# Graph layer of a two-block network: VectorE's copy into the padded stationary matrices moved behind the maxima over the neighbours in the second layer

## The chip, the cores and the metric

The kernel runs on one core of a Trainium2 chip. The metric is the device time of one execution in microseconds, the median over several runs. Before the change it is 1098.5 us (three runs, 1095.35 to 1098.69).

The engines are named as the profile names them: PE is TensorE's matmul and PEld its weight load, DVE is VectorE, ACT is ScalarE, POOL is GpSimd, SP is SyncE, which only issues DMAs here.

## The reference, cut to what matters

The program is a chain of six residual parts on an activation `x` of 2 x 64 x 1024: a quantised product, a state-space block, a feed-forward part with routed low-rank additions, a graph network over point clouds, a masked linear layer and a gated feed-forward part. The change lies in the graph network, `_L1_xattn_ref`. There are two clouds (the batch) of 1024 points, and two layers of this form:

```python
def _get_graph_features(feats, inds_list, perm, W_lin, b_lin, k=K):
    ...
    for inds in inds_list:
        neigh = gather(feats, inds)
        gf = jnp.concatenate([jnp.broadcast_to(center, (B, N, k, C)), neigh - center], axis=-1)
        per_method.append(gf)
    ...
    scores = jnp.einsum('bihd,bjhd->bhij', qh, qh) / np.float32(np.sqrt(headdim))
    attn = jax.nn.softmax(scores, axis=-1)
    out = jnp.einsum('bhij,bjhd->bihd', attn, qh).reshape(B * N, k, total)
    fused = out @ W_lin.T + b_lin
    return fused.reshape(B, N, k, 128)
...
g2 = _get_graph_features(feats1.transpose(0, 2, 1), inds_list, perm2, W_lin2, b_lin2)
h2 = jnp.einsum('oc,bnkc->bonk', W_conv2, g2)
h2 = _lrelu(_instance_norm(h2, (2, 3)))
feats2 = h2.max(axis=-1)
```

Every point has K = 10 neighbours in each of four orders of the points along curves. For every point the 10 neighbours attend to one another, the result goes through two linear maps (64 output channels in the first layer, 128 in the second), is normalised over all points and neighbours of a cloud, and the largest value over the neighbours is kept.

## The kernel before, in words

**Tiling.** The graph network works through *items*. An item is 48 neighbouring points of one cloud and one layer (the last item of a cloud is smaller: 16 points, or half the columns). A cloud has 22 items; the order is layer 1 cloud 0, layer 1 cloud 1, layer 2 cloud 0, layer 2 cloud 1, 88 items in all. Points are packed three at a time into blocks of 32 columns (30 used), so a full item has 16 blocks and its attention scores are one 128 x 512 tile.

**The software pipeline.** All engine queues in this part are in the order in which the program issues instructions; no scheduler reorders them. The function `iteration(i)` (L1281) issues one step, in which up to seven items are in work at different stages. A step issues, in this order:

- on POOL, `edges` of item i+2 (L999): the differences between neighbours and centre points, `x`, from the arrays `win` and `cen`, 128 x 960 elements; just before or after it stand gathers (`sl`, L948), indirect DMAs that POOL issues to fetch rows of the next cloud;
- `apart` of item i+1 (L1011 and L1013): `x` is copied into `xz`, a matrix padded with zeros, in which the two 64-row halves stand apart so that it can serve TensorE as a stationary matrix. Half 1 is copied by DVE in layer 2 (L1011), and by ACT in layer 1 except for the very first item; half 0 is copied by ACT (L1013), later in the step;
- `turn` of item i-2 (L1048): DVE transposes the normalised attention weights `e` in 32 x 32 blocks into `at`. It needs POOL's product of an earlier step (L1044);
- `collect` of item i-4 (L1113, L1115): DVE takes statistics (`st`) and maxima over the neighbours (`hm`) from the PSUM tile `pt`, which TensorE's back-transposition (L1102) wrote at the end of the step before. `pt` has one buffer, so the next back-transposition must wait for the maxima. After a cloud's last item `finish` adds the normalisation to the plan;
- `exponentials` of item i-1 on ACT (L1037), `scores` of item i on PE (L1019, L1022);
- `normalize` of item i-1: DVE sums the exponentials into `z` (L1042) and takes the reciprocal (L1043), and POOL multiplies `e` by it (L1044);
- `maxima` of item i: DVE takes the largest score (`mx`, L1027) and, in layer 2, subtracts it (L1030);
- `apart` half 0 of item i+1 on ACT, `attend` of item i-3 on PE (L1089, L1092) with ACT's copy `oT` (L1094), `weighted` of item i-1 on PE (L1073 in layer 2) with ACT's copies `u` (L1075), `turn_u` (L1079, layer 1 only), and `back` of item i-3 on PE (L1102).

Side work from a list with due times (`plan`, run by `todo`) is issued between these: the gathers, the placing of gathered rows (L955, L960, L965), the terms of the centre points (`crest`, `ct`, L920 and L927 on DVE), the Newton steps of a normalisation (L159 to L170), leaky ReLU (L1184), and, near the end, POOL's products that mask a weight of the next layer (L1395, `w_attn`).

**Order on DVE in one step of layer 2.** Copy (L1011), `at` (L1048), `st` (L1113), `hm` (L1115), `z` (L1042), reciprocal (L1043), `mx` (L1027), `e` (L1030), then side work. **Order on POOL.** Gather if one is due, `x` of item i+2 (L999), gather if one is due, product (L1044), masked weight if due (L1395).

**Buffers.** `x` and `xz` have four buffers each, the scores two in PSUM, `pt` one.

Of the kernel before, what the change touches and what calls it, by code (L numbers as in the profile page):

```python
# [92 lines left out]
class Kernel:  # L93
# [1093 lines left out]
    def point_cloud(self):  # L1187
        nc, tc, a = self.nc, self.tc, self.a
        with ExitStack() as es:
# [63 lines left out]
            at = lambda i: items[i] if 0 <= i < last else None  # L1253

            def todo(i):
                while plan and plan[0][0] <= i:
                    plan.pop(0)[1]()
# [16 lines left out]
            def edge(i):  # L1274
                it = at(i)
                if it:
                    it["pu"] = []
                    it["x"], it["xz"] = x16[i % len(x16)], xz[i % len(xz)]
                    self.edges(it)

            def iteration(i):  # L1281


                todo(i - 0.5)
                edge(i + 2)
                todo(i - 0.25)
                if at(i + 1):
                    self.apart(at(i + 1), 1)
                if at(i - 2):
                    self.turn(at(i - 2))  # L1290
                if at(i - 4):
                    it = at(i - 4)
                    ph, end = it["ph"], it["last"]
                    self.collect(it)
                    if end:
                        work = self.finish(ph)
                        if work:
                            plan.extend((i + k, w) for k, w in enumerate(work))
                            plan.sort(key=lambda e: e[0])
                if at(i - 1):  # L1300
                    self.exponentials(at(i - 1))
                if at(i):
                    self.scores(at(i))
                if at(i - 1):
                    self.normalize(at(i - 1))
                if at(i):
                    self.maxima(at(i))
                if at(i + 1):
                    self.apart(at(i + 1), 0)
                if at(i - 3):  # L1310
                    self.attend(at(i - 3))
                if at(i - 1):
                    self.weighted(at(i - 1))
                    self.turn_u(at(i - 1))
                if at(i - 3):
                    self.back(at(i - 3))
                todo(i)

            for i in range(-2, last + 3):
                iteration(i)  # L1320
# [8 lines left out]
            for q in range(2):  # L1329
                part(q, slice(0, P), w3, feats, start=True)  # L1330
                part(q, lo, w3a, phases[0]["out"])
                part(q, hi, w3a, phases[1]["out"])
                part(q, lo, w3b, phases[2]["out"], stop=True)
            iteration(last + 3)
            for q in range(2):
                part(q, hi, w3b, phases[3]["out"], stop=True)
# [204 lines left out]
```

## Time and profile before

One execution was profiled. It spans 1105.6 us from the first to the last instruction, and took 1107.58 us, 9 us more than the median of the runs shown; the mean granted clock of TensorE was 0.970.

| what | us |
|---|---|
| median of three runs | 1098.5 |
| profiled execution, time | 1107.58 |
| profiled execution, span | 1105.6 |
| steps that issue the 44 second-layer copies, first to last copy's start | 739.96 to 1003.49 |
| chain of waits, share of PE | 45% |
| chain of waits, share of DVE | 28% |
| chain of waits, share of POOL | 7% |
| chain of waits, share of the copy L1011 over the whole chain | 3% |

How such lines are read. A line of the groups names the source line, engine and operation, then output and inputs with their shapes, the number of instances, the busy time and the mean length of one in ns, and last the idle time of the engine in front of them with what ended most of it. A line of the timeline has the start, the length, the engine, the line, the operation and its tiles; an entry in brackets is idle time ahead of it. In a table by stretches each number is the busy time of one engine in that stretch. An instruction that stands still inside itself counts as busy.

### The profile page before, as it was taken

The numbers are of one execution on the slowest core, as the hardware profiler recorded it, in microseconds if no ns is written. First come the engines' busy times: TensorE is split into PE (matmuls) and PEld (weight loads), VectorE is DVE, ScalarE is ACT, GpSimd is POOL, SyncE is SP. The second block draws the span as 40 slices with busy tenths as digits, with TensorE's granted clock in tenths as the row PEclk, the third lists the DMA queues.
The fourth block names the chain that finished last, engine by engine and source line by source line (L and its number), as shares of the span: only waits on it lengthen the run. The fifth ranks groups of instructions, "written<-read, shape, count | busy, mean of one in ns | idle before, by whom it ended". The sixth has DMA issues, their size and how long they took to land.

```text
span 1105.6 us, 34714 instructions
## 1 busy us (share of the span) xinstructions
PE 990.0 (90%) x15287; PEld 736.7 (67%) x15287; DVE 800.3 (72%) x1667; ACT 604.7 (55%) x988; POOL 511.9 (46%) x425
## 2 busy tenths in 40 slices
PE   3899989999999999894788879889899899999997
PEld 1798949688696867453455545558777788887443
DVE  6698975776777676343588888889988689998411
ACT  6334416665756743113677767667877677775010
POOL 0010110102162446226999979888667577882000
PEclk9999999999999999895999999999999999999999
DMA  9777758695866957455031003110323200000550
GB/s 345 259 293 289 308 207 328 233 425 210 365 267 268 382 211 284 161 170 102 17 69 29 13 11 70 22 32 15 56 39 94 90 14 12 9 4 3 218 238 20
DMA packets 49027, 170.93 MB, mean 155 GB/s; under 512 B 26551, under 2 KB 27491, under 8 KB 42093
## 3 DMA queue, kind: packets, MB, share of 16 engines
q1 hardware_dynamic: 38988, 151.83, 37.0%
q10 hardware_dynamic: 3744, 12.65, 3.4%
q0 software_dynamic: 6144, 4.24, 2.2%
q8 instruction: 120, 1.97, 0.7%
q14 instruction: 31, 0.25, 0.1%
HBM read 163.48 MB, written 2.72 MB: 150 GB/s over the span
## 4 chain that ended last, share of the span: by engine, by line
PE 45%; DVE 28%; POOL 7%; ACT 7%; DMA 6%; issue 6%; ACTq 0%; DVEq 0%; SPq 0%; POOLq 0%
PE pin L369 11%; PE po L506 7%; PE misc L1073 6%; POOL sl L948 3%; DVE cpre L384 3%; PE op L1092 3%; PE sc L1422 3%; DVE xz L1011 3%; DMA sl<-src,place 2%; DMA df<-in_L_attn_mask 2%; POOL e L1044 2%; POOL x L999 2%; PE misc L1422 2%; DVE z L1042 2%; DVE mx L1027 2%
## 5 line engine op out<-in xcount | busy, mean ns | idle before, releaser
L369 PE MATMUL pin<-hT,w 128*128 128x128 f32 x2320 | 263.3, 275 | 1.2 <-issue 0.8
L369 PEld LDWEIGHTS pin<-hT,w 128*128 128x128 f32 x2320 | 261.0, 192 | 4.9 <-issue 4.2
L999 POOL TENSOR_TENSOR x<-win,cen 128x960 f16<-128x960 f32 (+1 forms) x88 | 170.3, 1935 | 4.4 <-ACT win L965 3.0
L1013 ACT COPY xz<-x 64x1024 f16<-64x1024 f16 (+1 forms) x131 | 133.6, 1020 | 15.3 <-POOL x L999 11.3
L948 POOL DMA_INDIRECT sl<-src,place x128 | 129.0, 1007 | 25.5 <-issue 14.3
L1073 PE MATMUL misc<-wz,xz 128*64 128x128 bf16 x4128 | 129.1, 220 | 6.1 <-issue 2.6
L1073 PEld LDWEIGHTS <-xz 128*64 128x64 f16 x4128 | 118.7, 110 | 18.0 <-issue 17.0
L1044 POOL TENSOR_TENSOR e<-e,z 128x512 f32<-128x512 f32 x88 | 91.0, 1034 | 76.6 <-DVE z L1043 63.4
L483 POOL TENSOR_TENSOR xc<-y,normw 128x512 f32<-128x512 f32 x8 | 8.3, 1037 | 243.4 <-DVE y L481 200.8
L1075 ACT COPY u<-misc 128x512 f32<-128x512 f32 x172 | 97.1, 587 | 32.5 <-PE misc L1073 24.3
L799 ACT ACTIVATE df<-df,neg 128x1024 f32<-128x1024 f32 x64 | 73.4, 1148 | 75.6 <-DVE df L798 66.3
L506 PE MATMUL po<-ow,xc 128*128 128x512 f32 x240 | 109.8, 611 | 0.0
L384 DVE SCALAR_TENSOR_TENSOR cpre<-craw,convw,cpre 128x126 f32<-128x126 f32 (+2 forms) x240 | 80.6, 357 | 24.3 <-ACT cpre L378 18.6
L782 POOL DMA_INDIRECT place<-cst,rank x64 | 66.2, 1035 | 51.5 <-DVE rank L804 23.7
L1092 PE MATMUL op<-u,at 128*32 128x64 f32 (+1 forms) x2752 | 84.5, 256 | 3.4 <-issue 3.1
L798 DVE SCALAR_TENSOR_TENSOR df<-hi_r,hl,lo_r 128x1024 f32<-128x1024 f32 x64 | 80.8, 1292 | 3.2 <-DMA lo_r<-rows 1.5
L506 PEld LDWEIGHTS po<-ow,xc 128*128 128x128 f32 x240 | 46.1, 197 | 53.3 <-issue 52.5
L1048 DVE STREAM_TRANSPOSE at<-e 128x512 f32<-128x512 f32 x88 | 61.1, 694 | 20.3 <-POOL e L1044 19.6
L1022 PEld LDWEIGHTS <-xz 128*64 128x64 f16 x2752 | 51.6, 114 | 34.7 <-issue 32.6
L1062 PE MATMUL misc<-x,heads 128*32 128x512 f16 (+1 forms) x1056 | 73.4, 395 | 1.2 <-issue 0.5
L1042 DVE TENSOR_REDUCE z<-e 128x16 f32<-128x512 f32 x88 | 58.0, 659 | 19.5 <-ACT e L1037 19.2
L1092 PEld LDWEIGHTS op<-u,at 128*32 128x32 f32 x2752 | 61.3, 113 | 14.1 <-issue 6.9
(364 smaller groups left out, 1557.9 us busy)
## 6 DMA issues: line engine op xcount, KB each, us to landing
w<-in_in_proj_w SPq DMA_DIRECT2D x36, 2048.0 KB
ow<-in_out_proj_w SPq DMA_DIRECT2D x16, 2048.0 KB
w<-in_L_ffn_w SPq DMA_DIRECT2D x3, 4096.0 KB
ow<-in_ctx SPq DMA_DIRECT2D x4, 1024.0 KB
w<-in_ctx SPq DMA_DIRECT2D x4, 1024.0 KB
hi_r<-rows ACTq DMA_DIRECT2D x8, 512.0 KB
lo_r<-rows ACTq DMA_DIRECT2D x8, 512.0 KB
df<-in_L_attn_mask ACTq DMA_DIRECT2D x8, 512.0 KB
```

What stands on the lines that cost most here:

```text
L369: nc.tensor.matmul(pt[:, c, :], w[:, c, kc, :], hT[:, kc, :], start=(kc == 0), stop=(kc == KC - 1))
L384: nc.vector.scalar_tensor_tensor(pv[:, :, s:], rv[:, :, :S - s], convw[:, cc + c, 3 - s:4 - s], pv[:, :, s:], ALU.mult, ALU.add)
L506: nc.tensor.matmul(st["pq"][n], st["xc"][:, 4 * q + c, :], ow[:, c, 512 * n:512 * n + 512], start=(q == 0 and c == 0), stop=(q == 1 and c ...
L798: V.scalar_tensor_tensor(df, hi_r, hl[:, 0, cc:cc + 1], lo_r, ALU.subtract, ALU.add)
L948: nc.gpsimd.indirect_dma_start(out=ph[c][:, m, :], out_offset=None, in_=ph["src"][:, :], in_offset=bass.IndirectOffsetOnAxis(ap=k, axis=0))
L999: nc.gpsimd.tensor_tensor(xv[:, :, r0:nb], over, mid, ALU.subtract)
L1013: nc.scalar.copy(dst, src)
L1042: nc.vector.tensor_reduce(z, e, AX.X, ALU.add)
L1044: nc.gpsimd.tensor_tensor(e, e, z.unsqueeze(2).to_broadcast([P, nb, 32]), ALU.mult)
L1073: nc.tensor.matmul(pu[64 * hp:64 * hp + 64, k, :], xz[:, hp, k0 + k].rearrange("p a j -> p (a j)"), wz[j][:, hp, :], start=(j == 0), stop= ...
L1075: nc.scalar.copy(u[:, k0:k0 + kb], pu)
L1092: nc.tensor.matmul(op[32 * r:32 * r + 32, q, :], it["at"][:, 4 * q + r, :], it["u"][:, 4 * q + r, :], start=False, stop=True, skip_group_c ...
```

## The change

DVE's half of `apart` is taken out of its place at the head of the step for items of layer 2 and issued after `collect` and `finish`, in front of `exponentials`. For items of layer 1 it stays where it was (there it is ACT's copy, with one exception, the very first item).

```diff
                 todo(i - 0.25)
-                if at(i + 1):
+                if at(i + 1) and at(i + 1)["layer"] == 1:
                     self.apart(at(i + 1), 1)
                 if at(i - 2):
                     self.turn(at(i - 2))
...
                             plan.extend((i + k, w) for k, w in enumerate(work))
                             plan.sort(key=lambda e: e[0])
+
+                if at(i + 1) and at(i + 1)["layer"] == 2:
+                    self.apart(at(i + 1), 1)
                 if at(i - 1):
                     self.exponentials(at(i - 1))
```

In DVE's compiled queue the 44 copies then stand behind `at`, `st` and `hm` and in front of `z`. The other instructions of DVE, and those of PE, ACT, POOL and SP, keep their order. The copy no longer carries a wait for POOL; the transposition in front of it carries one. Lines behind the inserted ones, about L1300 on, have numbers higher by 3 in the changed kernel; all the lines named above but L1395 stand before it.

## The prediction, made before the changed kernel was run

> **What bounds the kernel now.** I read the page's busy line first, then the stretches in which the second graph layer runs, then VectorE's and GpSimd's timelines inside them, and last the chain of waits. The page's first line:
>
> ```profile
> PE 990.0 (90%) x15287; PEld 736.7 (67%) x15287; DVE 800.3 (72%) x1667; ACT 604.7 (55%) x988; POOL 511.9 (46%) x425
> ```
>
> TensorE's 90% is an average. The change touches 44 copies of the second layer, started between 740 and 1003 us. Busy times there (columns: stretch, length, then PE, PEld, DVE, ACT, POOL busy, clock, DMA):
>
> ```profile
> 740.00:760.00 20.00, 17.46 (x528) 13.28 (x530) 19.11 (x36) 12.22 (x24) 18.78 (x16) 1.00 0.08 15
> 760.00:782.00 22.00, 19.25 (x577) 16.52 (x567) 21.09 (x49) 17.52 (x30) 14.76 (x12) 1.00 0.06 12
> 812.00:851.00 39.00, 36.98 (x1008) 30.93 (x1002) 34.82 (x53) 29.11 (x52) 26.34 (x20) 1.00 0.13 29
> 922.00:949.00 27.00, 26.58 (x789) 22.74 (x784) 25.33 (x44) 20.67 (x37) 25.19 (x19) 1.00 0.07 15
> 949.00:1003.00 54.00, 51.57 (x1529) 44.01 (x1526) 52.66 (x69) 38.94 (x68) 42.03 (x28) 1.00 0.02 5
> ```
>
> So TensorE is near full in some stretches (26.58 of 27) and VectorE in others (52.66 of 54). In the latter VectorE is full partly because it stands still. Groups kept apart by shape, 740 to 1003:
>
> ```profile
> L999 POOL TENSOR_TENSOR x<-win,cen 128x960 f16<-128x960 f32 x40 | 79.8, 1995 | 0.6
> L1011 DVE COPY xz<-x 64x1024 f16<-64x1024 f16 x42 | 47.6, 1134 | 1.1
> ```
>
> The copy's shortest full instances take 0.42 us, so 42 of them should take 17.6; about 30 us are waiting inside the instruction. The timeline says for whom:
>
> ```profile
> 958.02 1.05 POOL L1044 TENSOR_TENSOR e<-e,z 128x512 f32<-128x512 f32 x1
> 958.02 5.12 DVE L1011 COPY xz<-x 64x1024 f16<-64x1024 f16 x1
> 959.02 1.91 POOL L1395 TENSOR_TENSOR w_attn<-w_attn,on 128x1024 f32<-128x1024 f32 x1
> 960.89 1.96 POOL L999 TENSOR_TENSOR x<-win,cen 128x960 f16<-128x960 f32 x1
> ...
> 967.00 1.91 POOL L1395 TENSOR_TENSOR w_attn<-w_attn,on 128x1024 f32<-128x1024 f32 x1
> 967.16 2.05 DVE L1011 COPY xz<-x 64x1024 f16<-64x1024 f16 x1
> 968.88 2.15 POOL L999 TENSOR_TENSOR x<-win,cen 128x960 f16<-128x960 f32 x1
> ```
>
> Each blocked copy ends 0.30 us after a GpSimd instruction does (963.14 after 962.85; 969.21 after 968.91): it cannot run beside one. The chain of waits between 949 and 1001 goes through copy, transposition and VectorE's issue in every step, so there this blocking is the step time (6.05 us from copy to copy).
>
> **The change, part by part.** Nothing is added or removed. Forty-four copies, on VectorE alone, move behind three neighbours in its queue: the transposition of the weights (L1048), the statistics (L1113) and the maxima over neighbours (L1115). No DMA moves. The copy's own wait for GpSimd goes, since the transposition in front now waits for a later GpSimd product.
>
> Its users: TensorE's scores read it a step later. At 882.76 a copy begins whose scores begin at 889.77; 3 us later is still in time, cost nothing. TensorE's back-transposition (L1102) needs the maxima to have freed its PSUM buffer, so it may go up to one copy (0.42 to 2 us) earlier: a gain where it waited (0.2 to 0.46 us a step near 965 to 983). Queued behind the copy are now the sums z (L1042), the reciprocal and GpSimd's product (L1044), which waits for them: that decides.
>
> Where does the copy arrive? One undisturbed step, VectorE and GpSimd interleaved:
>
> ```profile
> 800.37 0.67 DVE L1042 TENSOR_REDUCE z<-e 128x16 f32<-128x512 f32 x1
> 801.47 1.05 POOL L1044 TENSOR_TENSOR e<-e,z 128x512 f32<-128x512 f32 x1 [0.33 <-DVE z L1043]
> 802.63 0.50 DVE L1011 COPY xz<-x 64x1024 f16<-64x1024 f16 x1
> 802.67 0.99 POOL L948 DMA_INDIRECT sl<-src,place  x1
> 803.14 0.71 DVE L1048 STREAM_TRANSPOSE at<-e 128x512 f32<-128x512 f32 x1
> 803.68 1.97 POOL L999 TENSOR_TENSOR x<-win,cen 128x960 f16<-128x960 f32 x1
> 804.88 0.66 DVE L1042 TENSOR_REDUCE z<-e 128x16 f32<-128x512 f32 x1
> ```
>
> Before, the copy slips in ahead of the gather (802.63 against 802.67) and takes 0.50; z to z is 4.51 us. After, transposition, statistics and maxima (0.63 + 0.55 + 0.55 us) come first, so the copy arrives at z + 4.0, inside x, which began at z + 3.31 and ends at z + 5.28. With the 0.30 us that follow a release, next z is at z + 5.60. A closed loop has come about: **z, product, gather, x, copy, z = 5.60 us**, against TensorE's own step of 5.56 (scores at 925.20 and 930.76). Where VectorE used to catch up at 4.5 us a step it no longer can; where TensorE leads, the loop just fits beside it and costs nothing.
>
> By stretches:
> - **740 to 782** (layer change; GpSimd busy 18.78 of 20). Steps were 4.1 to 5.1 us. At the first, the product ends at 741.03, the shortened collection brings the copy to about 742.33, and x starts at 742.19: it loses by 0.14 and waits to 744.17 + 0.3. The first four z, at 742.57, 746.72, 751.26 and 755.94, become 744.5, 750.1, 755.2 and 760.8 (5.6 us a step, the half-size item a little less). +4.9, of which an unblocked copy at 766.54 (0.77) returns 0.4: **+4.5**. If the copy won that 0.14 us, only each x would be 0.43 later: about +1.
> - **782 to 812**: VectorE at 5.6 us where it ran 4.5, TensorE busy 28.1 of 30 by its row: **+0.5**.
> - **812 to 851**: two copies of 2.71 and 2.72 us, blocked by gather and x, now fall free of both. TensorE has 39.0 - 36.98 = 2.0 us to give: **-2.0**, ends 0 and -3.
> - **851 to 900**: VectorE waits 0.9 to 3.0 us a step for TensorE: **0**.
> - **900 to 949**: one copy of 1.90 goes free (-1.4), given back because three steps of 4.4 to 5.0 become 5.6: **0**, ends -1.4 and +1.5.
> - **949 to 1003**: GpSimd also multiplies the masked weight (L1395). Before, the copy waited for it and got in ahead of x, though x was next (x stretched to 2.15). The loop becomes 1.10 + 1.00 + 1.87 + 1.97 + 0.33 = 6.27 us against 6.05: six steps, +1.3, and entering it +0.9: **+2.2**. The other end: the copy gets in before x, and TensorE's 5.56 takes over, -3.
> - **after 1003**: no more x; TensorE idles 1.4 of 17 us, of which half comes back: **-0.7**.
>
> Sum 4.5 + 0.5 - 2.0 + 2.2 - 0.7 = **+4.5 us**. The profiled execution spans 1105.6 us (1107.58 as timed), 9 above the median of the runs, 1098.5; the sum is a difference inside that execution, and I add it to the median: **1103.0 us**.
>
> **A rule against the row.** The last stretch hangs on who gets in when the copy arrives at z + 4.01 and the weight product ends at z + 4.01 (973.06 + 1.91 - 970.96). The Trainium skill, "SBUF — State Buffer", section "Who interferes with whom", says that VectorE and GpSimd share a port pair as an exclusive lock, and that whichever issues first holds it for its whole instruction. By it a copy pending before x goes ahead of x, a step falls to TensorE's 5.56, and the stretch gives -3: the sum would be -0.7. The rows agree with the lock, but not with first come: the copy of 958.02 was overtaken by two GpSimd instructions begun after it, and one at 791.77 lost to an x recorded 0.07 us later and took 2.34. I take the row: a near tie is lost. The same page's summary advises putting whichever of the two is off the critical path behind; here the blocked one is moved in front of what GpSimd waits for, which speaks against the change.
>
> **Rivals.**
> - Faster: the copy wins its races. Layer change +1, 812 to 851 -2, batch change -1.4, last stretch -3, end -0.7: -6, **1092.5 us**. Five copies pending during the weight product did win. The point is the order of arrival: 0.14 us earlier at the layer change, some 0.05 at the end. Against it: ordinary steps arrive 0.7 us too late.
> - No difference: TensorE's 5.56 hides the loop's 5.60 everywhere but where gains and losses cancel; **1098.5**. For it, 26.58 of 27 busy; against it, TensorE idles 5.3 of the first 42 us.
> - Slower still: two loops within 1% of each other lose slack at each uneven step (positions, centres, Newton's steps). 0.15 us in 30 more steps: +9, **1107.5**.
> - That the move is not made can be left out: VectorE's compiled queue shows it.
>
> **Numbers.** Forecast 0.45, still slower 0.17, no difference 0.18, faster 0.20. This kernel's runs spread over 0.3%, so within 3.3 us counts as the same. Almost all of the first two lie above: slower 0.60, same 0.20, faster 0.20. The stretches' ends added give about -6 and +10; cut to 8 in 10: 1093 to 1109. The forecast alone spans 1101 to 1106.
>
> **What would show it.** Right: copies of 1 to 1.6 us ending 0.3 us after an x; z to z of 5.6 in steps that took 4.1 to 4.5; 6.3 from 965 on; GpSimd's products waiting longer for the reciprocal. Wrong: copies at 0.42 with x stretched instead, steps of 5.6 in the last stretch, or TensorE waiting for the copy in the scores.

## The result, and the profile after

The changed kernel takes 1102.74 us (median of 13 runs, 1099.8 to 1115.07); the kernel before takes 1096.1 us in as many runs beside it (1092.85 to 1105.42). The ratio is **1.0065, 95% interval 1.0041 to 1.0089**: slower, by 7.1 us (4.5 to 9.8).

The execution that was profiled is the shortest of its 13 (span 1097.7 us, time 1099.8 us), while the one of before was a long one (1107.58 us). Its last sum in front of the moved copies (L1042, called z41 below) comes 9 us earlier than in before (728.20 for 737.23), by code that the change does not touch. So the two spans cannot be set against each other; the way from one sum z to another can. The busy line of the changed kernel's page:

```profile
PE 976.4 (89%) x15287; PEld 726.6 (66%) x15287; DVE 804.4 (73%) x1667; ACT 604.4 (55%) x988; POOL 511.2 (47%) x425
```

No engine's work has changed: the counts are the same, VectorE's busy time is 4.1 us higher (800.3 before). The stretches of the changed kernel that lie 9 us earlier than the first two and the last two rows shown of before; the first two are as far behind z41 as there, and hold less of the work, since the steps are longer (stretch, length, then PE, PEld, DVE, ACT, POOL busy, clock, DMA):

```profile
731.00:751.00 20.00, 16.36 (x459) 12.62 (x450) 18.60 (x31) 10.20 (x20) 16.25 (x13) 0.83 0.06 13
751.00:773.00 22.00, 17.77 (x524) 15.09 (x520) 21.06 (x46) 16.12 (x30) 14.21 (x12) 1.00 0.05 11
913.00:940.00 27.00, 26.28 (x785) 22.47 (x781) 26.37 (x40) 19.60 (x36) 21.88 (x18) 1.00 0.06 12
940.00:994.00 54.00, 49.57 (x1457) 42.39 (x1453) 50.04 (x70) 37.62 (x66) 42.16 (x28) 1.00 0.02 5
```

The clock of 0.83 in the first row does not set its time: in a second execution of the changed kernel it was 0.91 in the same place, with the same steps (44.95 us in the table below for 44.92). In the first two rows, the 42 us of the layer change, TensorE is busy 34.13 us where it was 36.71, and GpSimd does 30.46 us of work where it did 33.54: both wait more. VectorE stays as full as it was (39.66 of 42; 40.20 before), since a copy that stands still counts as busy. The same two groups of the changed kernel, between 731 and 994 us:

```profile
L999 POOL TENSOR_TENSOR x<-win,cen 128x960 f16<-128x960 f32 x40 | 78.8, 1971 | 0.7
L1011 DVE COPY xz<-x 64x1024 f16<-64x1024 f16 x42 | 52.9, 1259 | 1.3
```

The 42 copies took 47.6 us and take 52.9 here, and 50.0 and 49.9 in two more executions of the changed kernel. So only a few us more are spent standing still. What changed is **how it is spread and where it stands**: the median copy took 499 ns and takes 1388 now, and the longest, which was 5.12 us, is 2.20. An ordinary step of the changed kernel, from its timeline:

```profile
773.12 0.69 DVE L1042 TENSOR_REDUCE z<-e 128x16 f32<-128x512 f32 x1
...
774.24 1.05 POOL L1044 TENSOR_TENSOR e<-e,z 128x512 f32<-128x512 f32 x1 [4.57 <-DVE z L1043]
...
775.43 0.99 POOL L948 DMA_INDIRECT sl<-src,place  x1
...
776.44 1.97 POOL L999 TENSOR_TENSOR x<-win,cen 128x960 f16<-128x960 f32 x1
776.50 0.63 DVE L1115 TENSOR_REDUCE hm<-pt 128x48 f32<-128x480 f32 x1
777.16 1.54 DVE L1011 COPY xz<-x 64x1024 f16<-64x1024 f16 x1
778.57 0.97 POOL L948 DMA_INDIRECT sl<-src,place  x1 [0.16 <-issue]
778.74 0.69 DVE L1042 TENSOR_REDUCE z<-e 128x16 f32<-128x512 f32 x1
```

This is the forecast loop, closed: z at 773.12, product, gather, x to 778.41, copy to 778.70 (0.29 later), next z at 778.74: 5.62 us. The copy arrives at z + 4.04, where z + 4.0 was forecast. In the steps with a masked weight:

```profile
968.68 0.69 DVE L1042 TENSOR_REDUCE z<-e 128x16 f32<-128x512 f32 x1
...
969.80 1.05 POOL L1044 TENSOR_TENSOR e<-e,z 128x512 f32<-128x512 f32 x1 [1.43 <-DVE z L1043]
...
970.80 1.91 POOL L1398 TENSOR_TENSOR w_attn<-w_attn,on 128x1024 f32<-128x1024 f32 x1
...
972.68 1.96 POOL L999 TENSOR_TENSOR x<-win,cen 128x960 f16<-128x960 f32 x1
972.73 2.19 DVE L1011 COPY xz<-x 64x1024 f16<-64x1024 f16 x1
974.95 0.69 DVE L1042 TENSOR_REDUCE z<-e 128x16 f32<-128x512 f32 x1
```

z to z is 6.27 us: the copy comes 0.05 us after x has begun and waits for its end. The chain of waits in this stretch, by line, has the copy still in it, now together with GpSimd's work (changed kernel, 940 to 992 us, cut off at its end):

```profile
by line: DVE xz L1011 24.1%; POOL e L1044 12.2%; issue 10.6%; DVE at L1048 6.8%; DVE z L1042 6.7%; DVE hm L1115 6.4%; DVE st L1113 6.4%; PE misc L1073 4.5%; POOL sl L948 4.1%; POOL w_attn L1398 3.6%; ACT u L1075 3.0%; DVE z L1043 2.5%; ACT 
```

Before, in the same steps (949 to 1001 us), the copy had 37.4% and GpSimd's own lines none:

```profile
by line: DVE xz L1011 37.4%; issue 11.5%; DVE at L1048 10.9%; DVE z L1042 9.4%; DVE hm L1115 8.6%; DVE mx L1027 8.6%; DVE st L1113 8.5%; DVE z L1043 3.9%; ACT e L1037 1.0%; ACT pm L955 0.6%; DVE e L1030 0.6%
```

Over the whole chain GpSimd's share rose from 7% to 11%.

**The time between the same sums, us.** The stretches are named by the sums (z41 is the one ahead of the first moved copy in the changed order, z87 the last one). The "as before" columns are two profiled executions of the kernel before, the "as changed" columns three of the changed kernel, two of them from the experiments below.

| stretch, us of the profile before | as before | as changed | difference | forecast |
|---|---|---|---|---|
| z41 to z48 (737 to 778) | 40.56, 40.57 | 44.92, 44.95, 44.97 | +4.4 | +4.5 |
| z48 to z54 (to 812) | 34.70, 36.78 | 34.79, 38.67, 35.59 | unclear | +0.5 |
| z54 to z60 (to 852) | 39.54, 40.48 | 38.35, 40.18, 39.76 | unclear | -2.0 |
| z60 to z67 (to 897) | 44.48, 43.97 | 40.93, 44.91, 43.58 | unclear | 0 |
| z67 to z76 (to 950) | 53.18, 53.12 | 55.30, 55.31, 55.32 | +2.1 | 0 |
| z76 to z84 (to 1001) | 51.55, 51.54 | 50.39, 50.40, 50.40 | -1.15 | +2.2 |
| z84 to z87 | 12.72, 12.72 | 12.91, 12.90, 12.91 | +0.2 | -0.7 (with the next) |
| z87 to the end | 91.65, 90.34 | 91.93, 92.04, 91.65 | about +0.9, not settled | |

Four rows repeat to some 0.06 us from one execution to the next; three vary by up to 4 us within one kernel. In the first row the steps can be set side by side: from z41 the old order took 5.34, 4.15, 4.54, 4.68 and 5.68 us; the new one takes 7.24, 5.61, 4.91 (the half-size item), 5.61 and 5.62.

### The profile page after: what moved, and what is told of

Read it like the earlier page. It is cut to its first block, busy times and chain, and to the rows that moved or that the text cites. A ratio compares the mean times of both kernels' runs of the same rounds, so it can differ in the third digit from the quotient of the medians.

```text
span 1097.7 us, 34714 instructions
## 1 busy us (share of the span) xinstructions
PE 976.4 (89%) x15287; PEld 726.6 (66%) x15287; DVE 804.4 (73%) x1667; ACT 604.4 (55%) x988; POOL 511.2 (47%) x425
## 3 DMA queue, kind: packets, MB, share of 16 engines
q1 hardware_dynamic: 38988, 151.83, 37.4%
HBM read 163.48 MB, written 2.72 MB: 151 GB/s over the span
## 4 chain that ended last, share of the span: by engine, by line
PE 40%; DVE 30%; POOL 11%; ACT 7%; issue 6%; DMA 6%; ACTq 0%; DVEq 0%; SPq 0%; POOLq 0%
PE pin L369 11%; PE po L506 7%; PE misc L1073 4%; POOL sl L948 4%; POOL e L1044 4%; DVE xz L1011 3%; POOL x L999 3%; DVE cpre L384 3%; PE sc L1425 3%; DMA df<-in_L_attn_mask 2%; DVE z L1042 2%; DVE df L798 2%; PE misc L1425 2%; DMA sl<-src,place 2%; DVE at L1048 2%
## 5 line engine op out<-in xcount | busy, mean ns | idle before, releaser
L506 PE MATMUL po<-ow,xc 128*128 128x512 f32 x240 | 107.5, 600 | 0.0
L1102 PE MATMUL pt<-cst,oT 128*128 128x128 f32 x258 | 47.8, 294 | 33.1 <-DVE hm L1115 16.1
L1092 PE MATMUL op<-u,at 128*32 128x64 f32 (+1 forms) x2752 | 77.0, 254 | 0.0
L1042 DVE TENSOR_REDUCE z<-e 128x16 f32<-128x512 f32 x88 | 58.6, 666 | 16.5 <-ACT e L1037 15.1
L1062 PE MATMUL misc<-x,heads 128*32 128x512 f16 (+1 forms) x1056 | 67.9, 393 | 0.0
```

The source lines that it names most:

```text
L506: nc.tensor.matmul(st["pq"][n], st["xc"][:, 4 * q + c, :], ow[:, c, 512 * n:512 * n + 512], start=(q == 0 and c == 0), stop=(q == 1 and c ...
L1042: nc.vector.tensor_reduce(z, e, AX.X, ALU.add)
```

## The experiments

All ratios are to the kernel before on the same chip; the absolute times differ between chips by over 1% (1096.1, 1110.9 and 1109 us for the same kernel), so only ratios and stretches are compared.

**Both kernels once more, unchanged**, to see which stretches repeat.

> The kernel before once more, for a second profile, since two single executions are being compared stretch by stretch. Step numbers are those of the sums z (L1042), z41 is the last before the first moved copy. If the loop through x is the cause, z41 to z48 and z79 to z84 repeat within 0.3 us (40.6 us, and 6.06 us a step), and only the stretch z60 to z67, where the first profile has 44.5 us with VectorE waiting for TensorE, comes out some 3 us shorter. If the stretches differ between executions by several us everywhere, single profiles cannot carry the account.

> The changed kernel once more. Loop theory: z41 to z48 again 44.9 us, steps of 5.62 us where nothing else is late, 6.27 us in the stretch of the masked weight, each copy ending 0.3 us after an x. Theory of chance: the equal steps of 5.62 do not come back.

One execution each: 1108.27 us for before, 1116.75 us for the changed one. The stretches of the layer change, of the batch change and of the masked weights repeat to 0.05 us and are in the table. The stretches between z48 and z67 do not. Of the kernel before, z60 to z67 was expected some 3 us shorter than in its first profile, and is 0.5 us shorter. The same stretch, 3.5 us shorter in the first profile of the changed kernel than in that of before (40.93 against 44.48), is 44.91 against 43.97 here, so that gain was none of the change's; and z48 to z54 is 3.9 us longer than in the changed kernel's first profile. In these stretches TensorE stands still within a series of its matmuls, for a time that differs from one execution to the next, while no engine and no transfer of this loop is named as its releaser. In the changed kernel's second execution:

```profile
810.12 0.65 PE L1022 MATMUL sc<-x,xz 128*64 128x32 f16 x30 [1.88 <-issue]
```

and in the first profile of the kernel before, 0.99 us:

```profile
804.13 0.65 PE L1022 MATMUL sc<-x,xz 128*64 128x32 f16 x30 [0.99 <-issue]
```

So a difference in these three stretches of a single pair of profiles is no evidence on the change.

The traces hold a candidate for these pauses. In all fourteen executions profiled, those of over 0.6 us between z41 and z87 lie at two places, z52 or z53 and z61 (one execution has only the second). Each of them ends 2.2 to 3.4 us after a transfer on the queue that the page lists as `q8 instruction` has begun: 804.13 after 800.95 in the kernel before, 810.12 after 806.72 in the second execution of the changed one. Code that arrives late would explain them, but 58 such transfers stand in this part of each trace, at least 55 of them with no such pause, and no run here tests it. The granted clock goes along in z48 to z54 (1.00 for 34.70 and 0.95 for 36.78 us before), but z54 to z60 varies from 38.35 to 40.48 us at a clock of 1.00.

**The changed kernel timed again**, beside the next three.

> The changed kernel on the same chip as the two halves: 1.0065 again, within 1.004 to 1.009, and z41 to z48 of 44.9 us for a third time. By every theory that adds up over the steps, the two halves sum to it.

1.0063 (1.0034 to 1.0091): the result repeats.

**The move in the first six steps alone, and in all others alone.** The place of the loss is tested by giving each part of the layer its own order.

```diff
-                if at(i + 1) and at(i + 1)["layer"] == 1:
+                if at(i + 1) and not 44 <= i + 1 < 50:
                     self.apart(at(i + 1), 1)
...
-                if at(i + 1) and at(i + 1)["layer"] == 2:
+                if at(i + 1) and 44 <= i + 1 < 50:
                     self.apart(at(i + 1), 1)
```

> The new order for the first six items of the second layer only (44 to 49, the layer change), the old order for the other 38. Loop theory and its account by stretches: this stretch holds most of the loss, z41 to z48 again 44.9 us instead of 40.6; the later stretches are those of before (z67 to z76 53.1, z76 to z84 51.5). Ratio to before 1.003 to 1.005. Rival 'the place in front of z' (the same small cost in every step): 6 of 44 steps, so 1.001 and not to be seen.

> The counterpart: old order for items 44 to 49, new order for the other 38. Account by stretches: z41 to z48 40.6 us as before, z67 to z76 2.1 us longer, z76 to z84 1.1 us shorter; between, lost catching up. Ratio to before 1.000 to 1.004. Rival 'the place in front of z': nearly the whole loss, 1.0055.

For "all but the first six", the two conditions are turned round (`i + 1 < 50`, `i + 1 >= 50`). Six moved copies give **1.0045 (1.0026 to 1.0063)**, and their profile has 44.95 us from z41 to z48 with every later repeatable stretch as before (53.26, 51.53, 12.72). The other 38 give **0.9995 (0.9979 to 1.0012)**, just under the expected 1.000 to 1.004, with 40.59 in the first stretch and 55.32 and 50.39 later, as in the changed kernel. So the layer change carries the loss, 4 to 5 us of it, and the rest of the layer is worth nothing that can be told from zero. The rival that each of the 44 copies costs a little (+9 in 30 more steps) falls: it put the 38 copies at 1.0055. The two halves add up to 1.0040, which lies below the 1.0063 of the whole and within its interval.

**The copy behind the reciprocal**, so that z and the product no longer stand behind it.

```diff
-
-                if at(i + 1) and at(i + 1)["layer"] == 2:
-                    self.apart(at(i + 1), 1)
                 if at(i - 1):
                     self.exponentials(at(i - 1))
...
                 if at(i - 1):
                     self.normalize(at(i - 1))
+                if at(i + 1) and at(i + 1)["layer"] == 2:
+                    self.apart(at(i + 1), 1)
```

> The copy stands one place further back, behind z and the reciprocal, in front of the largest score. Loop theory: the copy no longer stands between x and the sums that GpSimd waits for; it begins 0.87 us after z, before the product (1.10), so it takes 0.42 us in most steps and the product starts 0.2 to 0.35 us later; steps fall to TensorE's 5.56, z41 to z48 loses about 4 us against the changed kernel. Ratio to before 0.993 to 1.000, some 7 to 12 us below the changed kernel. Rival 'the copy delays the scores' (they read it next): this is later still, so slower than the changed kernel, above 1.0065. Rival 'only the place in front of z counts, not the blocking': the time of before, ratio 1.000.

1.0032 (1.0013 to 1.0052): lower than the changed kernel's, but not at or under 1.000 as expected. Two parts of the expectation came out: nearly all copies run free (median 425 ns), and with masked weights most steps are TensorE's 5.56 us (z76 to z84 is 48.95). The miss is in the copies that are not free. Five are held for over 1 us, two of them at the layer change (2.17 and 1.70 us), where z41 to z48 takes 43.45 us: 1.5 less than in the changed kernel, not the expected 4. The longest is held in the steps of the masked weight:

```profile
972.13 6.00 DVE L1011 COPY xz<-x 64x1024 f16<-64x1024 f16 x1
973.01 1.04 POOL L1044 TENSOR_TENSOR e<-e,z 128x512 f32<-128x512 f32 x1
974.02 1.90 POOL L1397 TENSOR_TENSOR w_attn<-w_attn,on 128x1024 f32<-128x1024 f32 x1
975.89 1.95 POOL L999 TENSOR_TENSOR x<-win,cen 128x960 f16<-128x960 f32 x1
...
978.19 0.27 PE L1022 MATMUL sc<-x,xz 128*64 128x32 f16 x6 [1.62 <-DVE xz L1011]
```

It came while an x that began at 971.09 ran, and was passed by three GpSimd instructions that began after it. And since the copy now stands at the end of what VectorE does for a step, TensorE has caught up with it: the scores wait 1.62 us for it here, 2.5 us in three places together, and the weight loads 5.0 us in six. Besides, where VectorE no longer sets the pace TensorE falls due later: z84 to z87 takes 16.30 us for 12.72, 3.6 us more, where 2.6 were won with the masked weights.

**The copy behind the transposition**, in front of statistics and maxima: it arrives some 1.2 us earlier, during the gather.

```diff
                 if at(i - 2):
                     self.turn(at(i - 2))
+                if at(i + 1) and at(i + 1)["layer"] == 2:
+                    self.apart(at(i + 1), 1)
                 if at(i - 4):
```

> The copy stands behind the transposition alone, in front of the statistics. Loop theory: it arrives at z + 2.9, in the gather (z + 2.30 to 3.30), is overtaken by x and ends at z + 5.6; statistics and maxima now stand behind it, so next z is at z + 6.7 wherever a gather precedes x. With 20 to 30 such steps 15 to 30 us above before, ratio 1.014 to 1.027, slower than the changed kernel; with the masked weight in the way it gets in when that ends, 5.5 us a step. Rivals: 'the copy delays the scores' and 'the place in front of z' both make this equal to the changed kernel or faster, 1.002 to 1.0065.

1.0268 (1.0223 to 1.0312), as expected. A step of its timeline, which is the loop made longer by everything that the copy still has behind it:

```profile
790.11 0.69 DVE L1042 TENSOR_REDUCE z<-e 128x16 f32<-128x512 f32 x1
...
792.42 0.99 POOL L948 DMA_INDIRECT sl<-src,place  x1
...
793.03 2.67 DVE L1011 COPY xz<-x 64x1024 f16<-64x1024 f16 x1
793.43 1.97 POOL L999 TENSOR_TENSOR x<-win,cen 128x960 f16<-128x960 f32 x1
...
796.96 0.69 DVE L1042 TENSOR_REDUCE z<-e 128x16 f32<-128x512 f32 x1
```

The copy arrives within the gather (792.42 to 793.41), is held by it and then passed by x, and ends 0.30 us after x. Statistics and maxima then still stand in front of z: 6.85 us a step. This is the strongest sign for the loop: three places of one copy, with the same instructions on every engine, give steps of 4.5, 5.62 and 6.85 us, the last two being the loop through x with what stands between the end of x and the next z.

**Both gathers behind x**, in the changed and in the old order. Moving the gather away from in front of x should take 1.0 us out of where x stands.

```diff
-                plan.append((t - (0.25 if g % 3 == 1 else 0.5) * (t >= 0), gather(c, m)))
-            later = 0.5 * (g % 3 == 1)
+                plan.append((t - (0.25 if layer == 2 or g % 3 == 1 else 0.5) * (t >= 0), gather(c, m)))
+            later = 0.5 * (layer == 2 or g % 3 == 1)
```

> Changed kernel, with the second layer's gathers (and the copies that wait for them, half a step later) issued behind x instead of in front of it; the copy stays where the change put it. Loop theory: x now runs from z + 2.1 to z + 4.1 and the copy arrives at z + 4.0, so the loop is 4.4 us, TensorE's 5.56 governs and the slowdown goes except with the masked weight (6.27 stays): ratio to before 0.996 to 1.003, z41 to z48 below 42 us. Rival 'the place in front of z': the gathers' place is nothing to it, 1.0065 as the changed kernel.

> The same move of the gathers in the kernel before, where the copy still heads the step. Loop theory: the copy arrives at z + 2.26, just after x has begun (z + 2.1), waits to z + 4.4, and transposition, statistics and maxima stand behind it: next z at z + 6.1 in plain steps. Ratio to before 1.010 to 1.018, the opposite sign of the same edit in the changed kernel. Rivals: no effect, 1.000, since the copy is not in front of z and is early for the scores.

1.0147 (1.0112 to 1.0182) in the changed order, 1.0128 (1.0084 to 1.0172) in the old one. The second was expected, the first was not. In the changed order the copies do run free (median 426 ns where it was 1388), as the loop has it. But z41 to z48 takes 42.89 us, where less than 42 was expected, since the product in front of x pays for it. A step near 950 us:

```profile
950.38 0.69 DVE L1042 TENSOR_REDUCE z<-e 128x16 f32<-128x512 f32 x1
...
951.52 0.95 POOL L948 DMA_INDIRECT sl<-src,place  x1 [0.30 <-DVE z L1043]
...
952.48 1.06 POOL L1044 TENSOR_TENSOR e<-e,z 128x512 f32<-128x512 f32 x1
...
955.97 0.42 DVE L1011 COPY xz<-x 64x1024 f16<-64x1024 f16 x1
```

The second gather now stands in front of the product, so that the product begins 2.1 us after z, where 1.1 was usual. In the old order the copy arrives just inside x (817.57 against 817.42), takes 2.10 us, and z to z is 6.11. The edit costs in both orders, so it does not tell them apart: it moved the gathers into another wait. That freeing the copy pays cannot be read from it.

**A copy that cannot be blocked.** The sum z is a reduction, and it is not held up: beside an x it takes 0.66 us (804.88 in the kernel before). So the copy is written as a reduction over an axis of length one, which gives the same values, in the changed order and in the old one.

```diff
-            nc.vector.tensor_copy(dst, src)
+            if it["layer"] == 2:
+                nc.vector.tensor_reduce(dst, src.unsqueeze(4), AX.X, ALU.max)
+            else:
+                nc.vector.tensor_copy(dst, src)
```

> Changed kernel, the copy written as a maximum over an axis of length one: the same values by another VectorE instruction, in the same place. Loop theory, if such a reduction can run beside GpSimd as the reductions z, mx and hm do in every trace here: about 1.1 us each time (1024 elements at the 0.67 us that 512 take, less the fixed part), never ending 0.3 us after an x; VectorE's step 5.2 us, so TensorE's 5.56 governs also with the masked weight. Ratio to before 0.990 to 0.999. Rival 'the place in front of z': 0.7 us longer in front of z in each of 44 steps, slower than the changed kernel, 1.01 to 1.03.

> The same reduction in the kernel before, at the head of the step. Loop theory: 5.2 us a step on VectorE, no stall; as e7 within 0.3%, since without blocking the place hardly matters, 0.990 to 0.999. If it is e7 minus more than 0.5%, the place itself costs something beside the blocking.

All copies of the changed order, taken together (shortest, median and longest in ns, then first and last start):

```profile
L1012 DVE TENSOR_REDUCE xz<-x x44: 683/1216/1218, 745.8 to 1011.8; 64x1024 f16<-64x1024 f16 x42, 64x512 f16<-64x512 f16 x2
```

Median and longest are the same: not one was held up, beside an x or anything else. The price is 1.22 us where a free copy is 0.42. The changed order then gives 1.0023 (1.0005 to 1.0041), the old one 1.0004 (0.9986 to 1.0021). Both were expected below 0.999; the size was missed, since at the layer change 1.22 us is dearer than a copy that ran free (z41 to z48 42.19 in the old order, +1.6), and since, once the masked weights run at TensorE's pace (45.3 us for 51.5), z84 to z87 takes 15 to 16.3 us. What the pair does show: with nothing to block the copy, the two orders differ by about 0.2%, against 0.65% with it. About two thirds of the loss is the blocking, by these two ratios, whose intervals of 0.2% leave a good deal of room. The layer change alone has less of it: there the two reductions take 44.07 us in the changed order and 42.19 in the old one, so that 1.9 of the 4.4 us between the orders stay although nothing is blocked. 1.2 of them fall in the first step, which is taken up below.

**The reduction only where the copy was on the chain in before**, in the old order: the items from s = 12 on of the second cloud.

```diff
-            nc.vector.tensor_copy(dst, src)
+            if it["layer"] == 2 and it["b"] == 1 and it["s"] >= 12:
+                nc.vector.tensor_reduce(dst, src.unsqueeze(4), AX.X, ALU.max)
+            else:
+                nc.vector.tensor_copy(dst, src)
```

> A candidate: the kernel before, with the copy as a reduction only in the last ten items (layer 2, cloud 1, from its item 12 on), where the masked weight blocks it. Loop theory: z76 to z84 falls from 51.5 to about 45.4 us as in the two kernels that use the reduction everywhere, of which TensorE, now the bound, takes back some 3.5 us behind z84; the layer change stays at 40.6. Ratio to before 0.996 to 0.999. If blocking is worth nothing there because TensorE is the bound anyway: 1.000.

**0.9967 (0.9947 to 0.9987)**, 3.7 us faster than the kernel before, and so faster than both. A step with a masked weight:

```profile
974.67 1.91 POOL L1398 TENSOR_TENSOR w_attn<-w_attn,on 128x1024 f32<-128x1024 f32 x1
974.82 1.22 DVE L1012 TENSOR_REDUCE xz<-x 64x1024 f16<-64x1024 f16 x1
...
976.05 0.71 DVE L1051 STREAM_TRANSPOSE at<-e 128x512 f32<-128x512 f32 x1
```

A copy at this spot took 2.05 to 5.12 us in before; the reduction is not held, and the transposition follows at once. The chain between 949 and 1001 us, by line:

```profile
by line: PE misc L1076 48.0%; PE op L1095 18.1%; PE sc L1025 10.6%; PE pt L1105 9.0%; PE op L1092 5.7%; PE sc L1022 3.7%; issue 1.4%; PE misc L960 1.3%; ACT u L1078 1.2%; ACT pm L955 0.8%; ACTq L955 0.1%; ACTq L1040 0.0%; ACTq L1078 0.0%
```

The copy is gone from it and TensorE has nearly all. z76 to z84 takes 45.83 us for 51.54; of the 5.7 won, the next three steps give 3.6 back (16.31 for 12.72), because the work that TensorE was behind with is then what ends last.

## Why the prediction was right

The forecast was 1103.0 us, 4.5 more than the median it started from; measured were 1102.74 us, and 7.1 us (4.5 to 9.8) more by the ratio. That the time itself is met to 0.3 us is luck: the kernel before took 2.4 us less beside the changed one than the 1098.5 that the forecast started from, and the difference was 2.6 us more than forecast. The direction and the loop are shown. The sum by stretches is right partly because errors of opposite sign cancel, +2.1 and -3.35 us in two of them. The upper end of the range does not come out of the ends that the prediction lists: they add up to about +8, not +10.

- **The loop** of 5.60 us is 5.61 to 5.63 in the ordinary steps in which VectorE sets the pace, with copies that end 0.29 to 0.30 us after x. With masked weights 6.27 was worked out, and 6.27 or 6.28 is measured in five steps.
- **740 to 782, +4.5**: measured +4.4, and the six-step experiment gives 1.0045. The near tie was lost. The changed kernel's first moved copy, the product and the transposition ahead of it, and the x that it lost to:

```profile
730.92 1.05 POOL L1044 TENSOR_TENSOR e<-e,z 128x512 f32<-128x512 f32 x1
...
732.01 0.71 DVE L1048 STREAM_TRANSPOSE at<-e 128x512 f32<-128x512 f32 x1 [1.10 <-POOL e L1044]
...
733.14 1.97 POOL L999 TENSOR_TENSOR x<-win,cen 128x960 f16<-128x960 f32 x1
733.36 2.05 DVE L1011 COPY xz<-x 64x1024 f16<-64x1024 f16 x1
```

  It came 0.22 us too late, where 0.14 was worked out. The +1 of the rival needed it in time.

  The blocking is not the whole of this stretch. In the kernel before, the copy of this step ran while VectorE had to wait for the product anyway (739.97 to 741.03), and the transposition followed it at once:

```profile
739.96 1.36 DVE L1011 COPY xz<-x 64x1024 f16<-64x1024 f16 x1
741.33 0.71 DVE L1048 STREAM_TRANSPOSE at<-e 128x512 f32<-128x512 f32 x1
```

  In the new order VectorE is idle for 1.10 us until the product ends, and the copy comes on top. The step grew from 5.34 to 7.24 us; with the reduction, which nothing blocks, it is 5.20 us in the old order and still 6.42 in the new one. So some 1.2 of the 4.4 us come from a wait that the copy no longer fills. The next three steps (4.15, 4.54 and 4.68 us, now 5.62, 4.91 and 5.61) lost 2.8 us to the loop, and those behind them gave back 0.3. The prediction had this wait in its sum, through the time at which the copy arrives, and did not name it as a cost of the move.
- **782 to 812 (+0.5), 812 to 851 (-2.0), 851 to 900 (0)**: not settled one by one. Over four executions with each order in these steps (the changed order's include the one with all but the first six moved, the old order's those of the first six and of the late reduction), the means are 35.7, 40.0 and 44.1 us in the old order and 35.9, 39.3 and 43.4 in the new one: +0.2, -0.7 and -0.8, with 1 to 4 us from one execution to the next. The -2.0 is within that, but nothing shows it. The two copies of 2.71 and 2.72 us did go free (0.42 and 0.43 us), and their steps of 7.35 and 7.33 us became 6.38 and 6.09; two steps beside them rose, from 5.80 and 5.92 to 6.62 and 6.67.
- **900 to 949, 0**: mis-sized, measured +2.1. The copy that went free gave the 1.4 us (a step of 7.35 became 5.94). But three steps of 4.50, 5.01 and 4.91 us became 5.62, which is +2.4 and not the 1.4 that "given back" allowed; two steps at the batch change, of 5.14 and 6.15 us, became 6.14 and 6.56, and one of 6.00 gave back 0.4. The term was balanced to zero instead of summed. TensorE's 26.58 of 27 us made it look as if TensorE would hide the longer steps; the time of nine of them, 55.30 for 53.18, shows that it does not.
- **949 to 1003, +2.2**: mis-sized, measured -1.15. The five loops cost 0.22 each as worked out (+1.1). The step that leads in gave 1.6, since its copy found a gap: it began 0.01 us after the first masked weight ended (944.62 + 1.91) and ahead of the gather of 946.68, and ran free. The changed kernel:

```profile
946.54 0.42 DVE L1011 COPY xz<-x 64x1024 f16<-64x1024 f16 x1
947.00 0.69 DVE L1042 TENSOR_REDUCE z<-e 128x16 f32<-128x512 f32 x1
...
952.05 0.71 DVE L1048 STREAM_TRANSPOSE at<-e 128x512 f32<-128x512 f32 x1 [2.81 <-POOL e L1044]
...
953.90 2.19 DVE L1011 COPY xz<-x 64x1024 f16<-64x1024 f16 x1
```

  That step is 4.51 for 6.08; the one after it, in which the transposition waits for the product, is 9.13 in both kernels. The last step meets a half-size x and takes 5.38 for 6.06: that the cloud's last x is shorter was known and was left out of the six. The +0.9 for entering this part, for which the prediction shows no working, did not come: that is the step which gave 1.6.
- **The near tie there was taken as lost**, against the section "Who interferes with whom" of the Trainium skill's page "SBUF — State Buffer". It was lost: at 972.73 the copy came 0.05 us behind an x of 972.68. But there x had begun first, so the row does not speak against the page's "Whoever issues first". Other rows do: the copy of 958.02 before, and the one behind the reciprocal, which began first and was passed by three instructions. And others agree with it: in the kernel before, six copies (the prediction counts five) that began during the weight product got in ahead of the x behind it. So the order of issue decides in some of the cases here and not in others, and what else decides is open. The same section limits the exclusive lock to VectorE's two-port modes and instructions with two inputs, and says that a copy can enter such a mode and a reduction cannot; the held copies and the reductions of 1.22 us, none of them held, agree with that.
- **After 1003, -0.7**: wrong in sign: +0.2 up to z87. The +0.9 behind it rests on five executions with a spread of over 1 us, and is not settled.
- **"Products waiting longer for the reciprocal"**, named among the signs of a right forecast, did not come: in the group of the product, waits for z are 47.4 us in the changed kernel (731 to 994 us) and 52.3 before (740 to 1003). In the loop GpSimd's gathers, x and product take about 5 of the 5.62 us, so it has little time to wait; its wait is short in each step, and the step long. Its share of the chain is what rose.

Of the rivals, **no difference** is ruled out by the interval (1.0041 at its low end). **Faster** asked for copies that win their races. Two of its four places were lost (layer change, masked weights); the copies of 2.71 and 2.72 us and that of 1.90 us at the batch change went free, but longer steps beside them took back what they gave. **Slower still** gave +9, which the interval includes; its mechanism, a little in each of 30 more steps, falls with the 38 copies at 0.9995.

**What stays open.** The stretches add up to some +5.2 us (4.4 + 0.2 - 0.7 - 0.8 + 2.1 - 1.15 + 0.2 + 0.9), the ratio to 7.1 with an interval that begins at 4.5. The 2 us between them lie within the interval and within the scatter of the three stretches that do not repeat. What makes TensorE stand still in those was not tried, and neither was what lets a waiting copy in.

## What to carry to other kernels

Before an instruction that can be blocked is moved, look up in the timeline at what point of the other engine's work it will arrive at its new place, and what stands behind it in its own queue: 42 copies cost about as much standing still in both orders (47.6 and 52.9 us), and the loss came from a few steps in which GpSimd's product waited behind the blocked one, and from one wait that the instruction had filled at its old place and no longer fills. A loop that closes through two engines costs little where a third engine needs about as long (5.62 against 5.56 us), and its whole excess where that engine is not the limit, as behind a layer change, where full steps of 4.15 and 4.68 us became 5.6. Where two engines lock each other out, look for a form of the instruction that takes no part in the lock, and use it only where the wait is on the chain: everywhere it gained nothing (1.0004), in the last steps it gained 0.33%.

## What the runs showed of the hardware that had not been expected

- A VectorE copy that waits for GpSimd does not always keep its place. Three GpSimd instructions that began after it passed it in 6.00 us at 972.13 (copy behind the reciprocal), and an x that began 0.02 us behind the gather that held a copy passed that copy every time (2.67 us at 793.03, copy behind the transposition). But in the kernel before, the six copies that began 0.15 us into a masked weight ahead of an x got in before that x (2.05 us at 967.16). A held copy ends 0.28 to 0.30 us after an arithmetic instruction that held it, and 0.22 to 0.25 us after a gather (0.60 us at 839.87 in the changed kernel).
- The issue of an indirect DMA on GpSimd, 0.99 us, holds a copy only in its later part. A copy that arrives 0.61 us into it is held (793.03 in the gather of 792.42); one that arrives 0.29 us into it runs its 0.42 us (842.37 in the gather of 842.08, kernel before), and one that began 0.04 us before a gather took 0.50 us (802.63, same kernel). Among the gathers of about 1 us in all executions, copies up to 0.49 us in ran free, and from 0.53 us in none ended before the gather did.
- A VectorE reduction over an axis of length one copies the same 64 x 1024 elements beside GpSimd without being held: all 42 full ones took 1.22 us, in both orders (about 1.1 was expected), against 0.42 to 6.00 us for the copy.
- TensorE pauses for 0.7 to 3.0 us within one series of small matmuls, with no releaser in the trace, at the same two places of every execution but one, which has one of them. The length differs from one execution to the next. Single stretches of 35 to 45 us around them vary by up to 4 us, while others repeat to 0.05.
